# Feed-forward output product once per layer, from twelve-bit parts, accumulated in PSUM, with the gated blocks going by DRAM

## The chip, the cores and the metric

The kernel runs on one core of a Trainium2 chip. The metric is the device time of one execution in microseconds (us). Every kernel is also profiled once by the hardware profiler. The engines are named as in the profile: PE is TensorE (matrix products), PEld its weight loads, DVE is VectorE, ACT is ScalarE, POOL is GpSimd, and SP is the engine that issues most of the DMA transfers.

## The reference, cut to what matters

A graph network with four transformer layers (L = 4) over 1024 nodes of width 512. In each layer come an attention against a condition of 16 x 256 rows, and then a gated feed-forward block:

```python
for i in range(L):
    a = _attn(_ln(h, ln2_w[i], ln2_b[i]), cond, Wq[i], Wk[i], Wv[i], Wo[i])
    h = h + a
    u = _ln(h, ln3_w[i], ln3_b[i]) @ geglu_w[i] + geglu_b[i]   # 512 -> 4096
    val, gate = jnp.split(u, 2, axis=-1)
    f = val * jax.nn.gelu(gate, approximate=False)               # 1024 x 2048
    h = h + f @ ffo_w[i] + ffo_b[i]                              # 2048 -> 512
h = _gcn(h, src, dst, gcn_out_w, gcn_out_b, n)
```

The change concerns `f @ ffo_w[i]`: per layer a product of 1024 x 2048 by 2048 x 512, all in float32.

## The kernel before

It is written with a framework that records instructions in program order, allots tiles to a fixed number of buffers, adds all semaphores, and orders each engine's queue at compile time; `pin` (`keep_in_program_order`) and `in_order` fix the order of the instructions they hold. There are 36 large buffers ("slots", 128 x 1024 float32), 10 of half that size (`t512`), and eight PSUM banks of 128 x 512 float32. A tile that finds no free buffer waits until the last reader of an earlier one is done.

Two ways of multiplying float32 matrices are in use. The first is a plain float32 matmul, which shows in the profile as two records, in a Strassen-like scheme with 7 instead of 8 block products (`Quad`, `ffn_out`); its sums of blocks are computed beforehand and afterwards on DVE and POOL. The second is "twelve-bit": each operand is split into a high part, a low part and a combined part, of type fp32r, and three one-record matmuls take the place of a float32 one (`Twelve` for keys and values; `Chunk` for the gated projection). `left_parts` and `right_parts` make the parts: for 1024 columns one ACT multiplication, then DVE and POOL operations.

The feed-forward block of a layer goes through the 2048 columns of `f` in four quarters (`R = 4`, index `r`). The first quarter is made by four float32 `Quad`s (`c` = 0 to 3), while the pieces for the later quarters' right sides are split beside them: `fill()` takes one step of `begin_right` or `finish_right` at a time. The other three quarters are made by 12 `Chunk`s, whose steps are interleaved with those of the chunk before. In a chunk, `load()` fetches the geglu weights two chunks ahead (SP), `sum_chunk` adds their blocks (POOL), `split` makes their parts (ACT, DVE, POOL).

`Gated` holds one quarter of `f`, transposed, in four slots, and its Strassen sums (`sums`). As soon as a quarter is complete, `ffn_out(l, r, s, ...)` multiplies it by the quarter of `ffo_w` and adds it to the rows `h`: two calls per quarter (`s` = 0, 1, each for half of the rows), 28 float32 matmuls of 256 columns each. For `r` = 1 and 2 the two calls stand after chunks 0 and 1 of the next quarter; for `r` = 0 and 3 they follow one another. Each call's results are added to `h` and to `kept` by DVE (lines 1229, 1233 and 1245). `load_out` fetches the weights, `out_weights` makes their sums on POOL, and work for the next step is handed to `ffn_out` in `beside`. At a layer's end these are the splitting of `wk` and of `cond` for the next layer and the moments of the norm, after it that of `wv`. In the last layer it is followed by the aggregation over the graph, with `load_last` for its inputs.

The lines that matter in the profile: L1223 the matmuls of `ffn_out`; L1108 and L1170 those of a chunk (twelve-bit, and one float32 product); L296 those of the quads; L362 keys and values; L1011, L1029, L1030 the DVE work of a quad; L1042 and L1050 the steps of `begin_right` and `finish_right`; L1056 and L1059 the splitting of a chunk's left side; L1126 and L1143 a chunk's additions; L1082 a chunk's loads; L1192 and L1198 to L1200 the sums of `f`; L231 to L234 sums of blocks, among them those of `out_weights`; L313, L314, L316 `left_parts`; L324, L327, L334 `right_parts`; L759 the aggregation at the end.

Of the kernel before, what the change touches and what calls it, by code (L numbers as in the profile page):

```python
# [8 lines left out]
F32 = mybir.dt.float32  # L9
# [16 lines left out]
def gnn_kernel(  # L26
# [199 lines left out]
    cond_dram = dram.tile([NG, P, 4 * 512], F32, name="cond_dram")  # L226

# [81 lines left out]
    def left_parts(x, name):  # L309

        parts = [slots_of(2, f"{n}_{name}") for n in ("ah", "al", "as")]
        for h, l, s, x in zip(*parts, x):
            nc.scalar.mul(twelve_bits(h), x, INWARD * TINY)  # L313
            nc.vector.scalar_tensor_tensor(twelve_bits(l), h, -1.0 / TINY, x, OP.mult, OP.add)  # L314
            for k in range(2):
                nc.gpsimd.tensor_tensor(twelve_bits(s)[:, k, :], h[:, k, :], l[:, k, :],  # L316
                                        OP.subtract)
        return parts
# [643 lines left out]
    def load_out(l, r):  # L962
        return load_w(ffo_w[l][r * D:(r + 1) * D, :], f"wff_{l}_{r}")

# [12 lines left out]
    class Quad:  # L977
# [25 lines left out]
        def rest(self, fill):  # L1003
# [26 lines left out]
            pin(nc.vector.scalar_tensor_tensor(f1, d, bias, g1, OP.add, OP.mult))  # L1030
            fill()
# [35 lines left out]
    class Chunk:  # L1067
# [69 lines left out]
        def steps(self, sum_next):  # L1137
# [38 lines left out]
            pin(nc.vector.scalar_tensor_tensor(f1, d, bias, g1, OP.add, OP.mult))  # L1176

    class Gated:


        def __init__(self, l, r):
            self.n, self.tiles, self.s = f"{l}_{r}", [], None
# [6 lines left out]
        def sums(self, c, t=nc.vector, each=lambda ins: ins):  # L1189
            if c < 2:  # L1190
                a11, a21 = self.of(c)
                each(t.tensor_tensor(a21, a11, a21, OP.subtract))  # L1192
                return
            if c == 2:
                self.s = slots_of(3, f"fs_{self.n}")
            (a11, a21), (a12, a22) = self.of(c - 2), self.of(c)
            s1, s2, s4 = (x[:, c % 2, :] for x in self.s)
            each(t.tensor_tensor(s2, a22, a21, OP.subtract))  # L1198
            each(t.tensor_tensor(s1, s2, a11, OP.add))
            Gated.last = each(t.tensor_tensor(s4, a12, s2, OP.subtract))  # L1200

        def left(self):
            blocks = [[self.of(2 * j + k)[i] for k in range(2)] for i in range(2) for j in range(2)]
            return order7(blocks, *([x[:, k, :] for k in range(2)] for x in self.s))
# [5 lines left out]
    def ffn_out(l, r, s, left, right, kept, each=lambda ins: ins, beside=()):  # L1210

        n = f"{l}_{r}_{s}"
        u = kept[s]
        a, b, c, d = (bank(f"{x}_{n}") for x in ("fa", "fb", "fc", "fd"))
        h11, h12, h21, h22 = (hall[:, 4 * i + 2 * s:4 * i + 2 * s + 2, j * M:(j + 1) * M]
                              for i in range(2) for j in range(2))

        def product(i, to, start):  # L1220
            for q in range(2):
                for k in range(2):
                    each(nc.tensor.matmul(to[:, q * M:(q + 1) * M],  # L1223
                                          left[i][k][:, (2 * s + q) * P:(2 * s + q + 1) * P],
                                          right[i][:, k, :], start=start and q == 0 and k == 0,
                                          stop=q == 1 and k == 1, skip_group_check=True))

        def add(to, of):
            each(nc.vector.tensor_tensor(to, halves_of(of), to, OP.add))

        product(0, a, True)
        if r:
            each(nc.vector.tensor_tensor(u, a, u, OP.add))  # L1233
            for do in beside[2:3]:
                do()
        else:
            nc.scalar.copy(u, a)
        product(6, c, True)
        add(h22, c)
        product(4, d, True)  # L1240
        add(h22, d)
        for do in beside[3:]:
            do()
        product(5, b, True)
        each(nc.vector.tensor_tensor(u, b, u, OP.add))
        if r == R - 1:
            for to in (h22, h21, h12):
                add(to, u)
        for do in beside[:1]:
            do()  # L1250
        product(1, a, False)
        add(h11, a)
        for do in beside[1:2]:
            do()
        product(3, c, False)
        add(h21, c)
        product(2, d, False)
        add(h12, d)
# [134 lines left out]
    def load_last():  # L1393
        w = load_w(gcn_out_w, "w_out")
        pairs = slots_of(NB // 2, "base")
        for i, pair in enumerate(pairs):
            nc.sync.dma_start(pair, base_dram[2 * i:2 * i + 2].rearrange("n p d -> p n d"))
# [9 lines left out]
        return w, [pairs[nb // 2][:, nb % 2, :] for nb in range(NB)], again, row  # L1407
# [3 lines left out]
    with tc.issue_after(load_w.last.ins):  # L1411
        for d in range(NB):
            nc.sync.dma_start(c_dram[:, :, d, :].rearrange("s p n -> p s n"), by_sources(C[d]))
    for l in range(L):
# [217 lines left out]
        kept = [t512(f"kept_{l}_{i}") for i in range(2)]  # L1632
        raw_out = load_out(l, 0)
# [15 lines left out]
        def all_parts():  # L1649
            for i in (0, 1, 5, 6, 4, 3):  # L1650
                yield from begin_right(f"gt_{l}_{i}", *begun[i])
                if i < 2:
                    yield from finish_rights(i)
# [7 lines left out]
        for c, q in enumerate(quads):  # L1661
            q.rest(fill)
            if c == 0:
                with waiting_for(q.last, mybir.EngineType.Pool):
                    wff = out_weights(nc.gpsimd, l, 0, raw_out)
            f.sums(c, nc.gpsimd if c < 3 else nc.vector, pin)
        for _ in parts:
            pass
# [15 lines left out]
        load()  # L1684
        sum_chunk(0)
        def finish(*of):
            for _ in finish_rights(*of):
                pass

        def split_both():  # L1690
            split(0, False)
            split(0, True)

        finish(5)
        ffn_out(l, 0, 0, f.left(), wff, kept, pin, (lambda: finish(6), split_both))
        load()
        sum_chunk(1)
        ffn_out(l, 0, 1, f.left(), wff, kept, pin,
                (lambda: finish(4), lambda: (finish(3), split(1, False))))
        load()  # L1700
        raw_out = load_out(l, 1)

        def split_next(n):
            split(n, False)
            load()

        before = None
        for r in range(1, R):
            for c in range(KC):
                chunk = ready.pop(0)  # L1710
                flow = chunk.steps(lambda: sum_chunk(1))
                chunk.f = f if c else Gated(l, r)
                next(flow)
                if c > 2 or r == 1 and c or r > 1 and c == 0:
                    split_next(0)
                for step in range(3):
                    if before:
                        next(before, None)
                        if step == 2 and c == 0:
                            f.sums(KC - 1, nc.vector, pin)  # L1720
                    next(flow)
                output = r > 1 and c < 2
                if not output:
                    split(0, True)
                if c:
                    f.sums(c - 1, nc.vector, pin)
                before = flow
                if c == 0:
                    kept_f, f = f, chunk.f
                if output:  # L1730
                    ffn_out(l, r - 1, c, kept_f.left(), wff, kept, pin,
                            (lambda: split(0, True), lambda: split_next(1)))
                    if c == 1:
                        raw_out = load_out(l, r)
                if c == (KC - 1 if r + 1 < R else KC - 2):
                    wff = out_weights(nc.gpsimd, l, r, raw_out)
        for _ in range(3):
            next(before, None)
        f.sums(KC - 1, nc.vector, pin)
        fT = f.left()  # L1740
        if last:
            w_out, base, again, dinv_row = load_last()
            with waiting_for(Gated.last, mybir.EngineType.Pool):
                w_out = out_weights(nc.gpsimd, L, 0, w_out)
            ffn_out(l, R - 1, 0, fT, wff, kept)
        else:
            raw_wk = load_w(Wk[l + 1], f"wk_{l + 1}")
            load_cond(l + 1, 0)
            raw_wv = load_w(Wv[l + 1], f"wv_{l + 1}")
            wk = [[], [], []]  # L1750

            def split_wk(i):
                for part, t in zip(wk, right_parts(raw_wk[i:i + 1], f"wk_{l + 1}_{i}")):
                    part.extend(t)

            half = [0, 1, 4, 5], [2, 3, 6, 7]
            with in_order(mybir.EngineType.DVE):
# [19 lines left out]
    for nb in (0, 1, 4, 5):  # L1777
        into_parts(nb)
# [132 lines left out]
```

## Time and profile before

| | |
|---|---|
| median of 3 runs | 2386.01 us (2385.27 to 2387.61) |
| the profiled execution: its time | 2384.85 us |
| its span, first to last instruction | 2383.1 us |
| mean granted TensorE clock | 1.000 |
| DMA traffic | 138.32 MB, mean 58 GB/s |

How to read the rows that follow in the prediction. The page's first part gives each engine's busy time, its share of the span, and its instructions. A row of the grouped view names line, engine, operation, out<-in by tile names, shape and count; then the group's busy time and the mean of one in ns; then the idle time of the engine just before, and what ended it. A row of the view of one line gives for a group the least, median and greatest duration in ns. A row of the timeline gives start and length in us of neighbouring instructions of one kind, merged; matmuls overlap, so the distance of two starts is the time that the first one costs. A row of the view by windows gives the window, its length, and the busy time of PE, PEld and (without a filter by line) DVE, ACT and POOL with their counts, the granted clock, the mean share of the DMA engines and GB/s. A row of the waits gives who waited for whom, the sum in us, the number and the longest. A row of DMA issues gives the transfers, KB of each, and the median us from issue to landing.

### The profile page before, as it was taken

How to read it: one execution, taken by the hardware profiler on the slowest of the kernel's cores; microseconds unless marked ns; L12 is line 12 of the kernel's file. 1: busy time of each engine (PE TensorE's matmuls, PEld its weight loads, DVE VectorE, ACT ScalarE, POOL GpSimd, SP SyncE). 2: the span in 40 equal slices, each digit the busy share in tenths (PEclk: the TensorE clock that was granted, in tenths of full speed). 3: DMA queues.
4: the chain of work that ended last, by engine and by line, in shares of the span. 5: the costliest groups of instructions: out<-in, count | busy, mean ns of one | idle time of the engine just before them, and what ended most of it. 6: DMA issues, size and time to landing. Idle time of an engine off the chain costs nothing. (4 is left out here: it accounts for less than half of the span.)

```text
span 2383.1 us, 33689 instructions
## 1 busy us (share of the span) xinstructions
PE 2351.5 (99%) x12528; PEld 1769.3 (74%) x12528; DVE 1571.1 (66%) x3052; ACT 994.5 (42%) x2011; POOL 919.0 (39%) x815
## 2 busy tenths in 40 slices
PE   8999999999999999999999999999999999999999
PEld 5668886677777887577786888477786888567787
DVE  9874546887684455877794544867786544778764
ACT  7444444343344444343344444433334444434320
POOL 0142223565222224564512323555523224356531
PEclk9999999999999999999999999999999999999999
DMA  6041210111301101011211201021121111011140
GB/s 203 18 157 71 72 67 19 45 45 53 111 27 67 41 30 43 22 58 54 83 37 67 67 19 54 10 62 45 45 93 67 46 39 36 19 54 40 49 151 36
DMA packets 108844, 138.32 MB, mean 58 GB/s; under 512 B 8232, under 2 KB 65904, under 8 KB 108672
## 3 DMA queue, kind: packets, MB, share of 16 engines
q1 hardware_dynamic: 106576, 130.64, 17.0%
q0 software_dynamic: 1376, 4.30, 0.5%
q8 instruction: 104, 1.70, 0.3%
q10 hardware_dynamic: 720, 1.11, 0.1%
q14 instruction: 68, 0.56, 0.1%
HBM read 119.25 MB, written 16.78 MB: 57 GB/s over the span
## 5 line engine op out<-in xcount | busy, mean ns | idle before, releaser
L316 POOL TENSOR_TENSOR as_c<-ah_c,al_c 128x512 fp32r<-128x512 f32 x128 | 187.8, 1497 | 235.0 <-DVE al_c L314 228.9
L1122 ACT ACTIVATE g<-g 128x512 f32<-128x512 f32 x192 | 112.1, 584 | 280.0 <-PE g L1108 277.4
L373 ACT ACTIVATE v<-v 128x512 f32<-128x512 f32 x127 | 74.1, 584 | 220.5 <-PE v L362 218.3
L1059 POOL TENSOR_TENSOR gsa<-gha,gla 128x512 fp32r<-128x512 f32 x96 | 125.8, 1331 | 104.1 <-DVE gla L1056 104.1
L1059 POOL TENSOR_TENSOR gsb<-ghb,glb 128x512 fp32r<-128x512 f32 x48 | 70.1, 1461 | 218.6 <-DVE glb L1056 218.6
L362 PE MATMUL v<-bh_wv,ah_c 128*128 128x512 f32 x508 | 145.9, 409 | 0.0
L362 PE MATMUL v<-bs_wv,as_c 128*128 128x512 f32 x508 | 143.4, 404 | 0.0
L843 ACT ACTIVATE pr<-sc,nmax 128x256 f32<-128x256 f32 x256 | 118.1, 474 | 58.3 <-DVE nmax L838 58.3
L1108 PE MATMUL g<-gr,gsa 128*128 128x512 f32 x384 | 136.5, 436 | 0.0
L362 PE MATMUL v<-bl_wv,al_c 128*128 128x512 f32 x508 | 136.4, 390 | 0.0
L1135 ACT ACTIVATE g<-g,gcols 128x512 f32<-128x512 f32 x96 | 67.5, 703 | 164.8 <-DVE g L1143 161.6
L373 ACT ACTIVATE k<-k 128x512 f32<-128x512 f32 x125 | 72.6, 585 | 150.6 <-PE k L362 150.4
L362 PE MATMUL k<-ah_c,bh_wk 128*128 128x512 f32 x500 | 135.1, 392 | 0.0
L362 PE MATMUL k<-al_c,bl_wk 128*128 128x512 f32 x500 | 133.9, 390 | 0.0
L362 PE MATMUL k<-as_c,bs_wk 128*128 128x512 f32 x500 | 132.2, 395 | 0.0
L915 POOL TENSOR_TENSOR os<-oT 128x256 f32<-128x256 f32 x12 | 8.8, 734 | 318.8 <-DVE oT L889 291.5
L1223 PE MATMUL fa<-wff,fT 128*128 128x256 f32 x512 | 121.9, 381 | 6.7 <-DVE kept L1233 6.7
L1108 PE MATMUL g<-gr,gha 128*128 128x512 f32 x384 | 122.9, 401 | 0.0
L1108 PE MATMUL g<-gl,gla 128*128 128x512 f32 x384 | 119.0, 391 | 0.0
L1223 PEld LDWEIGHTS fa<-wff,fT 128*128 128x128 f32 x512 | 96.6, 190 | 26.7 <-DVE kept L1233 9.9
L378 DVE COPY kT<-k 128x512 f32<-128x512 f32 x54 | 37.3, 691 | 118.4 <-PE k L362 118.4
L362 PEld LDWEIGHTS v<-bs_wv,as_c 128*128 128x128 f32 x508 | 93.9, 188 | 24.2 <-issue 4.6
(368 smaller groups left out, 5875.6 us busy)
## 6 DMA issues: line engine op xcount, KB each, us to landing
ct<-cond_dram SPq DMA_DIRECT2D x48, 512.0 KB, 4.5
wff<-in_L_gnn_ffo_w_dram SPq DMA_DIRECT2D x32, 512.0 KB, 4.3
gxb<-in_L_gnn_geglu_w_dram SPq DMA_DIRECT2D x96, 128.0 KB, 2.2
gxa<-in_L_gnn_geglu_w_dram SPq DMA_DIRECT2D x96, 128.0 KB, 2.2
cond<-in_L_gnn_cond_dram SPq DMA_DIRECT2D x32, 256.0 KB, 3.5
cond_dram<-ct SPq DMA_DIRECT2D x16, 512.0 KB, 3.9
wk<-in_L_gnn_Wk_dram SPq DMA_DIRECT2D x8, 512.0 KB, 6.1
wv<-in_L_gnn_Wv_dram SPq DMA_DIRECT2D x8, 512.0 KB, 8.4
```

The lines of the kernel that those rows point to most:

```text
L316: nc.gpsimd.tensor_tensor(twelve_bits(s)[:, k, :], h[:, k, :], l[:, k, :], OP.subtract)
L362: pin(nc.tensor.matmul(self.bank, twelve_bits(left[k // 2])[:, k % 2, self.c * P:(self.c + 1) * P], twelve_bits(right[k // 2])[:, k % 2, : ...
L373: nc.scalar.mul(self.bank, self.bank, 1.0 + TINY)
L378: nc.vector.tensor_copy(self.to(), self.bank)
L843: nc.scalar.activation(pr3[:, a, :], ps3[:, a, :], AF.Exp, bias=nmax[:, a:a + 1], accum_out=tot[:, a:a + 1])
L915: t.tensor_tensor(s1, a21, a22, OP.add)
L1059: pin(nc.gpsimd.tensor_tensor(s_at, h_at, l_at, OP.subtract))
L1108: pin(nc.tensor.matmul(to, self.part(i, which)[:, k, :], self.rights[i][which].bitcast(F32R)[:, k, :], start=start and k == 0, stop=stop a ...
L1122: pin(nc.scalar.mul(to, to, 1.0 + TINY))
L1135: pin(nc.scalar.activation(to, of, AF.Gelu, bias=gcols[:, cg:cg + 1]))
L1223: each(nc.tensor.matmul(to[:, q * M:(q + 1) * M], left[i][k][:, (2 * s + q) * P:(2 * s + q + 1) * P], right[i][:, k, :], start=start and q ...
```

## The change

`ffn_out` with its Strassen sums goes, and so do `load_out` and the uses of `kept` and of `out_weights` for the layers. A class `Output` multiplies all of `f` by all of `ffo_w` once a layer, after the last chunk, without Strassen, from twelve-bit parts. Each finished block of `f` is stored to DRAM (`f_dram`) by two SP transfers. The output then runs over 16 units: two halves `s` of the rows by eight pairs of inner blocks. A unit fetches 512 KB of `f`, splits it (ACT once, DVE twice over 1024 columns), and multiplies 4 blocks of 128 rows. Each block of rows has two banks, `y` and `x`, that accumulate over all eight units; at the end of a half, DVE adds them to `h` with two operations per block. The weights' parts (24 slots) are made once and serve both halves: two of eight pairs during the last chunks, the others one per unit by `ahead`. The work for the next layer that stood beside `ffn_out` stands after units 8 to 14. In the first quarter, each piece of the right sides is now finished right after it is begun, and the first chunk is loaded after quad 1 and split after quad 2.

```diff
+    f_dram = dram.tile([2, DFF // P, P, 2, 256], F32, name="f_dram")
...
-    def left_parts(x, name):
+    def left_parts(x, name, t=None):
...
             nc.scalar.mul(twelve_bits(h), x, INWARD * TINY)
             nc.vector.scalar_tensor_tensor(twelve_bits(l), h, -1.0 / TINY, x, OP.mult, OP.add)
+            if t:
+                t.tensor_tensor(twelve_bits(s), h, l, OP.subtract)
+                continue
...
-        def sums(self, c, t=nc.vector, each=lambda ins: ins):
...
+        def store(self, c):
+            for s in range(2):
+                nc.sync.dma_start(f_dram[s, self.r * KC + c],
+                                  self.tiles[c][:, :, s * M:(s + 1) * M])
...
-    def ffn_out(l, r, s, left, right, kept, each=lambda ins: ins, beside=()):
...
+    class Output:
...
+        def fetch(self, n):
+            if n < 2 * UNITS:
+                s, u = divmod(n, UNITS)
+                self.raw[n] = slot(f"fr_{self.l}_{n}")
+                nc.sync.dma_start(self.raw[n], f_dram[s, 2 * u:2 * u + 2].rearrange(
+                    "c p i n -> p c (i n)"))
+        def split(self, n):
+            if n in self.raw:
+                self.f[n] = left_parts([self.raw.pop(n)], f"f_{self.l}_{n}", nc.vector)
...
+        def split_w(self, u):
+            x, name = self.raw_w.pop(u), f"wff_{self.l}_{u}"
+            h, l, s = self.w[u] = [slot(f"{n}_{name}") for n in ("bh", "bl", "bs")]
+            nc.scalar.mul(twelve_bits(h), x, INWARD / TINY)
+            yield
+            for k in range(2):
+                pin(nc.vector.scalar_tensor_tensor(
+                    twelve_bits(l)[:, k, :], x[:, k, :], 1.0 / TINY, h[:, k, :], OP.mult,
+                    OP.subtract))
+                yield
+                pin(nc.vector.scalar_tensor_tensor(
+                    twelve_bits(s)[:, k, :], h[:, k, :], -TINY, l[:, k, :], OP.mult, OP.add))
+                yield
...
+        def unit(self, n):
+            s, u = divmod(n, UNITS)
+            left, right = self.f.pop(n), self.w[u]
+            for b in range(4):
+                if u == 0:
+                    self.banks[b] = [bank(f"{x}_{self.l}_{s}_{b}") for x in ("fy", "fx")]
+                y, x = self.banks[b]
+                for which, to in enumerate((y, y, x)):
+                    for k in range(2):
+                        pin(nc.tensor.matmul(
+                            to, twelve_bits(left[which][0])[:, k, b * P:(b + 1) * P],
+                            twelve_bits(right[which])[:, k, :],
+                            start=u == 0 and which != 1 and k == 0,
+                            stop=u == UNITS - 1 and which != 0 and k == 1, skip_group_check=True))
+                if u == UNITS - 1:
+                    to = h[4 * (b // 2) + 2 * s + b % 2]
+                    nc.vector.scalar_tensor_tensor(to, y, 1.0 + TINY, to, OP.mult, OP.add)
+                    nc.vector.tensor_tensor(to, x, to, OP.add)
...
         def all_parts():
-            for i in (0, 1, 5, 6, 4, 3):
+            for i in SPLIT:
                 yield from begin_right(f"gt_{l}_{i}", *begun[i])
-                if i < 2:
-                    yield from finish_rights(i)
+                yield from finish_rights(i)
...
+        fetches = [(R - 2, 0), (R - 2, 3), (R - 1, 1), (R - 1, 3)]
+        splits = {(R - 2, 1): 3, (R - 2, 2): 2, (R - 1, 0): 3, (R - 1, 1): 2}
...
+            beside = {8: lambda: (fetch_next(), take_moments(l + 1, half[0], 0, 2)),
+                      9: lambda: split_of(wk, raw_wk, "wk", 0),
+                      10: lambda: split_of(wk, raw_wk, "wk", 1),
+                      11: lambda: (norm_first(), fetch_values()),
+                      12: lambda: split_cond(l + 1, 0),
+                      13: lambda: split_of(wv, raw_wv, "wv", 0),
+                      14: fetch_more}
+        with in_order(mybir.EngineType.DVE):
+            for n in range(2 * UNITS):
+                output.fetch(n + 2)
+                output.split(n + 1)
+                output.fetch_w(n + 4)
+                for _ in range(5):
+                    next(ahead, None)
+                output.unit(n)
+                beside.get(n, nothing)()
+            if not last:
+                split_of(wv, raw_wv, "wv", 1)
```

In the last layer the units 8, 9 and 13 are followed instead by the first half of the aggregation's parts (`into_parts`), by the fetch of the graph's counts (`load_counts`, POOL transfers into eight slots) and by that of the output weights; `load_base` follows the last parts.

237 lines of the change are left out of this document (96 added, 141 removed).

## The prediction

> **What bounds the kernel now.** I read the busy shares first.
>
> ```profile
> PE 2351.5 (99%) x12528; PEld 1769.3 (74%) x12528; DVE 1571.1 (66%) x3052; ACT 994.5 (42%) x2011; POOL 919.0 (39%) x815
> PEclk9999999999999999999999999999999999999999
> ```
>
> TensorE is busy 99% of the span at the full granted clock, and VectorE, the next engine, 66%. A change is therefore worth what it takes from TensorE's stream, less what TensorE newly waits for. Next come TensorE's waits (times in all, how often, the longest).
>
> ```profile
> PE fa L1223 <- DVE kept L1233: 6.7, 8, 0.8
> PE fd L1223 <- DVE fs L1199: 3.5, 8, 0.4
> PE gc L296 <- DVE gu L1011: 3.2, 4, 0.8
> PE g L1108 <- DVE g L1126: 1.0, 3, 0.3
> ```
>
> Line 1223 is the feed-forward output product, line 296 in these rows the gated projection's first quarter, line 1108 the chunks of the other three quarters. Three of the four waits stand at code that the change rewrites. Since matmuls overlap, I take their price from starts, not from busy time: the timeline of one call of `ffn_out` that waits, and line 1223's busy time by windows (all, a pair of calls, a waiting call, one that does not wait, another pair).
>
> ```profile
> 1072.85 1.89 PE L1223 MATMUL fa<-wff,fT 128*128 128x256 f32 x8
> 1074.57 1.89 PE L1223 MATMUL fc<-wff,fT 128*128 128x256 f32 x8
> 1076.30 0.59 PE L1223 MATMUL fd<-wffs,fs 128*128 128x256 f32 x2
> 1077.33 1.56 PE L1223 MATMUL fd<-wffs,fs 128*128 128x256 f32 x6 [0.43 <-DVE fs L1199]
> 1078.73 1.89 PE L1223 MATMUL fb<-wffs,fs 128*128 128x256 f32 x8
> 1081.45 1.99 PE L1223 MATMUL fa<-wff,fT 128*128 128x256 f32 x8 [0.83 <-DVE kept L1233]
> ...
> 1086.55 0.81 PE L1108 MATMUL g<-gr,gha 128*128 128x512 f32 x2
> ```
>
> ```profile
> 0.00:2383.10 2383.10, 395.12 (x1792) 338.88 (x1792) 1.00 0.18 58
> 1001.50:1025.60 24.10, 24.07 (x112) 21.02 (x111) 1.00 0.28 84
> 1072.80:1086.70 13.90, 12.58 (x56) 10.29 (x56) 1.00 0.14 39
> 1096.60:1108.70 12.10, 12.01 (x56) 10.51 (x56) 1.00 0.41 132
> 1197.60:1221.80 24.20, 24.14 (x112) 21.10 (x111) 1.00 0.10 36
> ```
>
> One of the seven products, four float32 matmuls of 256 columns at two records each, takes 1.73 us from start to start (1072.85 to 1074.57). A waiting call takes 1086.55 - 1072.85 = 13.70 us; busy 12.58 plus waits of 1.26 would be 13.84, so 0.1 of a call's busy time lies under its neighbour, and a call that does not wait is worth 12.01 - 0.1 = 11.9, a pair 24.0.
>
> **The change, part by part.**
>
> *TensorE, removed.* A layer has two pairs (first and last quarter), two waiting calls and two others: 2 x 24.0 + 2 x 13.70 + 2 x 11.9 = 99.2 us, in four layers 396.8. The row over the whole span, 395.1, agrees.
>
> *TensorE, added.* A layer has 16 units (two halves of the rows, eight pairs of inner blocks), each 4 blocks of rows x 3 parts x 2 = 24 twelve-bit matmuls of 512 columns: 384 a layer, 1536 in all. This operation is in the trace, in the chunks:
>
> ```profile
> 1028.10 0.63 PE L1108 MATMUL g<-gr,gha 128*128 128x512 f32 x2
> ...
> 1036.77 0.62 PE L1108 MATMUL g<-gr,gsb 128*128 128x512 f32 x2
> ```
>
> These are the first and the last of 20 rows of two matmuls: 38 matmuls in 8.67 us, 0.228 each, with nothing idle between. The new product costs 1536 x 0.228 = 350.5 us, 87.6 a layer and 5.48 a unit. TensorE's account is 350.5 - 396.8 = -46.3 us. The 0.228 holds only while its inputs are there, so the rest is a question of supply.
>
> *First quarter, gained.* `out_weights` and the Strassen sums of `f` leave GpSimd, which slows VectorE here:
>
> ```profile
> 978.44 1.71 POOL L231 TENSOR_TENSOR wffs<-wff 128x512 f32<-128x512 f32 x1
> 985.15 2.96 POOL L1192 TENSOR_TENSOR fT<-fT 128x512 f32<-128x512 f32 x2
> 987.50 1.16 DVE L1042 SCALAR_TENSOR_TENSOR gr<-ln3T,gt 128x512 fp32r<-128x512 f32 x1
> 989.19 0.67 DVE L1042 SCALAR_TENSOR_TENSOR gr<-ln3T,gt 128x512 fp32r<-128x512 f32 x1
> ```
>
> One form takes 1.16 us beside GpSimd and 0.67 without, and that lag makes the 0.8 us wait at `gc` once a layer. Eight of the twelve `finish_right` operations move from the first output calls into this stage, and the first chunk's split with them.
>
> ```profile
> L1011 DVE TENSOR_TENSOR gd<-gd,gu 128x512 f32<-128x512 f32 x16 | 11.1, 695 | 7.4 <-PE gd L296 7.4
> L1030 DVE SCALAR_TENSOR_TENSOR fT<-gd,gcols,g 128x512 f32<-128x512 f32 x16 | 11.8, 739 | 0.0
> ```
>
> ```profile
> 983.22 1.88 PE L296 MATMUL gb<-ln3S,ges 128*128 128x512 f32 x4
> 984.93 1.88 PE L296 MATMUL gc<-ln3T,wgate 128*128 128x512 f32 x4
> ```
>
> A quad on VectorE is then at most 5 additions and 5 fills at 0.69 and two of 0.74: 8.4 us against TensorE's 5 products at 984.93 - 983.22 = 1.71, 8.6. I book the 3.2 us as gained; if GpSimd's chunk sums keep the lag alive, it is 0.
>
> *Chunks, 0.* Additions and splits stay. VectorE loses the Strassen sums there and gets ten steps of weight splitting. The `f` stores, two a chunk, join SP's queue: behind a store that waits for `f1` stand the next chunk's loads, due a whole chunk later. If that margin goes, I allow up to 0.2 us a chunk, 10 in all, in the range only.
>
> *Output stage, supply.* VectorE and ScalarE must split each `f` unit and, up to unit 5, one pair of weight blocks. No such tile exists now; the nearest rows are the same code on other tiles.
>
> ```profile
> L314 DVE SCALAR_TENSOR_TENSOR al_c<-ah_c,ct x64: 1211/1217/2284, 100.1 to 1998.5; 128x1024 fp32r<-128x1024 f32 x64
> L1056 DVE SCALAR_TENSOR_TENSOR gla<-gha,gxa x48: 1211/1434/2312, 459.3 to 2275.5; 128x1024 fp32r<-128x1024 f32 x48
> L327 DVE SCALAR_TENSOR_TENSOR bl_wk<-wk,bh_wk x16: 679/683/1002, 94.9 to 1763.7; 128x512 fp32r<-128x512 f32 x16
> L313 ACT ACTIVATE ah_c<-ct 128x1024 fp32r<-128x1024 f32 x2 | 2.0, 1045 | 0.0
> ```
>
> (The first three give least, median and greatest ns.) A unit costs VectorE 2 x 1.22 + 4 x 0.68 = 5.2 us and ScalarE 2 x 1.05 = 2.1, under 5.48. At the contended 1.43 it would be 5.6, over by 0.1. I take the quiet price, because GpSimd has only four operations in this stage (`split_cond`). In the second half the weights are done; instead come eight accumulator reads of 0.69 (5.5), twelve pieces of `wk` and `wv` at 0.68 (8.2), two of `cond` at 1.22 (2.4), and moments and roots, which I estimate at 5, beside 8 x 2.44 = 19.5: 41 us against 43.8. It fits, narrowly. All eight PSUM banks belong to one half, but a block's two reads (1.4 us) match its six matmuls (1.37), so the second half can follow on.
>
> *DMA.* `f` goes out and back, 8.4 MB each way a layer, and in the first eight units 1 MB (`f` and weights) must land per unit, 1.05 MB / 5.48 us = 191 GB/s.
>
> ```profile
> ct<-cond_dram SPq DMA_DIRECT2D x48, 512.0 KB, 4.5
> wff<-in_L_gnn_ffo_w_dram SPq DMA_DIRECT2D x32, 512.0 KB, 4.3
> 2298.00:2312.00 14.00, 14.00 (x61) 11.27 (x60) 12.60 (x18) 1.41 (x2) 5.35 (x4) 1.00 0.93 337
> ```
>
> The last row (DMA share 0.93, 337 GB/s) shows room, and a fetch is issued two units, 11 us, ahead of a chain of 4.5 + 1.05 + 2.44 = 8.0 us. So 0, as long as a slot is free.
>
> *Seams, a loss.* After the last chunk `f0`, an addition and `f1` still stand on VectorE ahead of `split(1)`, and SP holds the last store ahead of `fetch(2)`. From the chunk's end I count 1.7 for those, 2.4 for `split(1)`, 2.7 for weights: the second unit is ready at 4.1 against 5.48, the third at about 9.3 against 11. Lower bound 0, upper one whole chain of 8; nearer the count, 1 us a layer, 4 in all. In the last layer 4 MB of counts join the fetches on the same DMA engines: 0 to 5, I take 2.
>
> **Sum.** The profiled execution took 2384.85 us (span 2383.1, 1.75 around it). 2384.85 - 46.3 - 3.2 + 4 + 2 = 2341.3. The median of the three runs is 1.2 higher, 2386.0, so I predict 2342 us, 44 us or 1.8% faster.
>
> **Rivals.** (A) *VectorE becomes the bound.* If GpSimd's work keeps its two-input operations at the contended price through the output stage (1.43, and 1.16 for 0.68), each of the first six units costs 2 x 1.43 + 4 x 1.16 = 7.5, 2.0 over, and the second half 5.5 + 12 x 1.16 + 18 x 1.43 + 5 = 50.2 against 43.8, 6.4 over: 18 us a layer, 74 in all, 2416; at half the overlap, 2379. For it: the 1.16 us row. Against: GpSimd is left with some 6 us in that stage. Chance 0.06, mostly at a part.
> The Trainium skill, page "SBUF — State Buffer", section "Who interferes with whom", says that a VectorE operation with two SBUF inputs and a reading GpSimd operation exclude each other completely. By that rule a 0.68 us operation behind a 1.71 us one would take up to 2.4, not the 1.16 seen, so the trace shows the conflict but not the whole of that price; it speaks against this change, which swaps accumulator additions for splits with two SBUF inputs.
>
> (B) *The slots run short, and the kernel gets slower.* Of 36 slots I count 24 for weight parts, 6 for `f` parts, 2 raw, 4 for the next layer at unit 8: exactly 36. If one is held longer, SP's queue stops at a fetch until the unit before has ended, and the fetch has one unit instead of two: 8.0 - 5.48 = 2.5 us of stall for each unit so hit. All 64 make 2342 + 160 = 2502; from 18 units on (44 / 2.5) the kernel is slower than before. For it: loads now wait for slots already.
>
> ```profile
> SPq L1082 <- PE g L1108: 399.1, 36, 21.9
> ```
>
> Against: the count closes at 36, and before and after unit 8 it is lower. Chance 0.09; a few units hit only cost 5 to 15.
>
> (C) *Every seam costs a whole chain*, 8 us instead of 1, because SP's store holds the fetches: 2342 + 28 = 2370. Chance 0.10. (D) *The product is no cheaper than it was*, since 190 ns of weight load per matmul are not hidden: 2342 + 1536 x 0.19 = 2634. The chunk rows load just as often at 0.228, so 0.01.
>
> **How the numbers follow.** The forecast has 0.74, with its own range 2334 (no seams at all: 2386 - 46.3 - 3.2 - 1.0, the `g` wait gone too, is 2335.5) to 2352. For eight in ten I go on to (C) and to small parts of (A) and (B): 2332 to 2364. About 0.2%, 4.8 us, is what a measurement of this kernel tells from no change. Faster: 0.74 + 0.10 and the parts of (A) and (B) that stay small, 0.02 each, together 0.88; within it 0.03, where these two eat the gain; slower 0.09, the rest of (A), 0.02, of (B), 0.06, and (D).
>
> **What would show it.** Right: 1536 new matmuls starting 0.228 apart with few waits; the `kept`, `fs` and `gc` waits gone; VectorE busy over 85% in the output stage without TensorE idle; 67 MB more of DMA bytes. Wrong: TensorE waiting in units for `f` parts (A, if VectorE is busy then; B, if a fetch or SP is late), or 5 to 8 us idle at the first units (C). A next layer that starts late, for want of `wk` or the norm, would be a miss of a step that I price at nothing.

## The result, and the profile after

The changed kernel takes 2390.49 us in the median of 13 runs (2388.59 to 2393.04); the kernel before took 2385.85 us in as many runs beside them (2384.96 to 2387.61). The ratio is 1.002, with a 95% interval of 1.0011 to 1.0028: 4.6 us slower, where 44 us faster was forecast. The profiled execution took 2390.05 us, its span is 2388.3.

The page of the changed kernel, its busy shares and the DMA bytes:

```profile
PE 2324.4 (97%) x12272; PEld 1722.9 (72%) x12272; DVE 1585.6 (66%) x3024; ACT 1082.1 (45%) x2099; POOL 794.7 (33%) x731
DMA packets 161068, 205.42 MB, mean 86 GB/s; under 512 B 11304, under 2 KB 101744, under 8 KB 160896
```

TensorE has 27 us less to do and stands idle longer. The waits of TensorE say for whom:

```profile
PE g L1110 <- ACT g L1124: 35.7, 20, 6.9
PE gc L297 <- DVE gu L1012: 6.3, 4, 1.6
PE g L1110 <- DVE g L1128: 3.0, 8, 0.4
PE fx L1255 <- DVE as_f L317: 2.0, 4, 0.5
```

(L1110 is the chunks' matmul that was L1108, L297 the quads', L1255 the new output product; L1124 scales a chunk's sums on ScalarE.) The `kept` and `fs` waits are gone. The `gc` wait doubled from 3.2 to 6.3, and a wait that was not there before, the chunks' for ScalarE, holds 35.7 us. The longest of these, 6.6 to 6.9, comes four times, once a layer.

To divide the whole difference I take, for every matmul record of a line, the distance to the next record's start, and set idle gaps above 0.15 us apart:

| stage (line before / after) | before, us | after, us | difference |
|---|---|---|---|
| output product (L1223 / L1255) | 386.6 + 10.2 waits | 351.4 + 2.0 waits | -43.4 |
| chunks, twelve-bit (L1108 / L1110) | 417.6 + 1.0 waits | 429.7 + 38.7 waits | +49.8 |
| chunks, float32 product (L1170 / L1172) | 64.6 | 63.1 | -1.6 |
| quads (L296 / L297) | 383.2 + 3.2 waits | 381.3 + 6.3 waits | +1.2 |
| all others | | | -0.9 |

The differences add up to 5.1, and the two profiled executions differ by 2390.05 - 2384.85 = 5.2. The product brought what it should; the same 1728 matmuls of the chunks cost 50 us more, 37.7 of them in waits and 12.1 in longer matmuls.

The windows of the second layer show where (columns as in the prediction): the first chunk in three parts, then the output stage.

```profile
1002.70:1014.60 11.90, 5.23 (x22) 3.65 (x21) 6.72 (x11) 4.21 (x8) 2.85 (x4) 0.90 0.47 136
1014.60:1019.10 4.50, 4.47 (x11) 3.54 (x12) 2.85 (x5) 0.36 (x1) 4.10 (x5) 0.51 0.02 5
1019.10:1023.57 4.47, 4.47 (x21) 3.68 (x20) 1.89 (x4) 3.90 (x7) 2.56 (x3) 1.00 0.00 0
1135.58:1223.87 88.29, 87.80 (x387) 72.16 (x386) 81.55 (x106) 27.19 (x27) 8.32 (x4) 1.00 0.49 170
```

And the first chunk of the kernel before:

```profile
1025.50:1037.23 11.73, 11.73 (x52) 9.50 (x51) 5.88 (x10) 6.63 (x12) 6.70 (x7) 1.00 0.16 45
```

The first chunk takes 20.87 us (1002.70 to 1023.57) instead of 11.73. TensorE is busy for 5.23 of the first 11.90 us, and then runs for 4.5 us at half the clock. In four layers that is 4 x 9.14 = 36.6 of the 49.8. The output stage, 88.29 us long with TensorE busy for 87.80, is as forecast.

What TensorE waits for in this chunk is read from the timelines backwards. TensorE, ScalarE, GpSimd, SP's queue and VectorE, in this order:

```profile
1007.32 0.61 PE L1110 MATMUL g<-gl,gla 128*128 128x512 f32 x2
1014.62 1.19 PE L1110 MATMUL g<-gr,gsa 128*128 128x512 f32 x2 [6.69 <-ACT g L1124]
```

```profile
1005.15 0.58 ACT L1124 ACTIVATE g<-g 128x512 f32<-128x512 f32 x1 [0.35 <-PE g L1110]
1012.46 1.06 ACT L1057 ACTIVATE gha<-gxa 128x1024 fp32r<-128x1024 f32 x1 [6.73 <-POOL gxa L1094]
1013.89 1.07 ACT L1124 ACTIVATE g<-g 128x512 f32<-128x512 f32 x2
```

```profile
1010.23 0.72 POOL L1094 TENSOR_TENSOR gxa<-gxa,gxb 128x256 f32<-128x256 f32 x1 [8.53 <-DMA gxa<-in_L_gnn_geglu_w_dram]
```

```profile
997.29 4.23 SPq L1084 DMA_DIRECT2D gxb<-in_L_gnn_geglu_w_dram  x4
1005.39 1.19 SPq L1194 DMA_DIRECT2D f_dram<-fT  x2
1006.68 2.16 SPq L1084 DMA_DIRECT2D gxa<-in_L_gnn_geglu_w_dram  x4
```

```profile
1004.63 0.74 DVE L1031 SCALAR_TENSOR_TENSOR fT<-gd,gcols,g 128x512 f32<-128x512 f32 x1
```

The last quad's piece of `f` is done at 1005.37 (1004.63 + 0.74). SP's queue holds the store of that piece (L1194) ahead of the second chunk's wide load `gxa` (L1084), so the load is issued at 1006.68 and has landed by 1010.23. GpSimd sums it, and ScalarE's next instruction in order is the wide split of the *second* chunk, at 1012.46; the first chunk's scaling (L1124), whose input had long been there, stands behind it, and TensorE needs its bank. One store that waits for its data stops an engine that is two queues away. In the kernel before, the second chunk's load stood at no store, and its split not inside the first chunk: between the quads and the first chunk stood the two output calls of the first quarter, 24.1 us of TensorE work (1001.50 to 1025.60 in the prediction's windows), and that split was made beside them. The change takes this stretch away.

### The profile page after: what moved, and what is told of

Its sections match the earlier page's. It is cut to its first block, busy times and chain, and to the rows that moved or that the text cites. A ratio compares the mean times of both kernels' runs of the same rounds, so it can differ in the third digit from the quotient of the medians.

```text
span 2388.3 us, 33592 instructions
## 1 busy us (share of the span) xinstructions
PE 2324.4 (97%) x12272; PEld 1722.9 (72%) x12272; DVE 1585.6 (66%) x3024; ACT 1082.1 (45%) x2099; POOL 794.7 (33%) x731
## 2 busy tenths in 40 slices
DMA packets 161068, 205.42 MB, mean 86 GB/s; under 512 B 11304, under 2 KB 101744, under 8 KB 160896
## 3 DMA queue, kind: packets, MB, share of 16 engines
q8 instruction: 102, 1.67, 0.3%
## 5 line engine op out<-in xcount | busy, mean ns | idle before, releaser
L320 POOL TENSOR_TENSOR as_c<-ah_c,al_c 128x512 fp32r<-128x512 f32 x128 | 195.3, 1556 | 416.8 <-PE fy L1255 242.1
L1110 PE MATMUL g<-gr,gsa 128*128 128x512 f32 x384 | 142.0, 452 | 35.7 <-ACT g L1124 35.7
L1255 PE MATMUL fx<-bs_wff,as_f 128*128 128x512 f32 x512 | 158.2, 390 | 2.0 <-DVE as_f L317 2.0
L1255 PE MATMUL fy<-bh_wff,ah_f 128*128 128x512 f32 x512 | 159.3, 392 | 0.0
L1255 PE MATMUL fy<-bl_wff,al_f 128*128 128x512 f32 x512 | 157.7, 389 | 0.0
L1124 ACT ACTIVATE g<-g 128x512 f32<-128x512 f32 x192 | 110.3, 581 | 99.3 <-PE g L1110 97.2
L314 ACT ACTIVATE ah_f<-fr 128x1024 fp32r<-128x1024 f32 x64 | 67.5, 1060 | 174.9 <-PE fy L1255 116.3
L1137 ACT ACTIVATE g<-g,gcols 128x512 f32<-128x512 f32 x96 | 67.5, 704 | 132.4 <-DVE g L1145 129.9
L1110 PEld LDWEIGHTS g<-gr,gsa 128*128 128x128 f32 x384 | 72.4, 194 | 76.1 <-issue 61.8
L1110 PE MATMUL g<-gr,gha 128*128 128x512 f32 x384 | 121.0, 396 | 0.0
L1110 PE MATMUL g<-gl,gla 128*128 128x512 f32 x384 | 118.8, 390 | 0.0
```

The costliest lines, as they stand in the source:

```text
L1110: pin(nc.tensor.matmul(to, self.part(i, which)[:, k, :], self.rights[i][which].bitcast(F32R)[:, k, :], start=start and k == 0, stop=stop a ...
L1124: pin(nc.scalar.mul(to, to, 1.0 + TINY))
L1137: pin(nc.scalar.activation(to, of, AF.Gelu, bias=gcols[:, cg:cg + 1]))
L1255: pin(nc.tensor.matmul(to, twelve_bits(left[which][0])[:, k, b * P:(b + 1) * P], twelve_bits(right[which])[:, k, :], start=u == 0 and whic ...
```

## The experiments

Each is the changed kernel with the edit shown, and its time is compared with the kernel before, run on the same chip beside it. My theory: the order of the queues at the seam from the quads to the chunks. The rival: VectorE is the bound there, or the new output stage costs what was lost.

**1. The second chunk's wide split behind the first chunk's steps**

```diff
-                split(0, False)
+                first = (r, c) == (1, 0)
+                if not first:
+                    split(0, False)
...
+                if first:
+                    split(0, False)
```

> Only the place of one call is changed: the wide half of the second chunk's split (ACT gha, DVE gla, POOL gsa) is issued after the first chunk's steps, not between its first two. Theory 1 (ACT's queue is in order, and the second chunk's gha, whose block sums on POOL are late, stands in front of the first chunk's copy gs and of the scaling): the 6.7 us wait of g for ACT in the first chunk goes in all four layers, with the slow clock behind it (0.51 for 4.5 us); the first chunk takes 11.7 to 12.5 us and not 20.9, and a smaller wait of 1 to 2 us may appear at the second chunk: some 28 to 36 us less, 2355 to 2363 us. Theory 2 (the late loads themselves hold the chunks, whatever stands in front of what): the wait moves to the second chunk in full, time within 5 us of 2390. Theory 3 (VectorE is behind with the right sides' pieces): no change.

Measured: 2381.43 us, ratio 0.9989 (0.9977 to 1.0), between the two expectations. The wait of the first chunk is gone, and one stands at the start of the second:

```profile
PE g L1110 <- ACT gha L1057: 13.1, 4, 4.2
```

So ScalarE's order made the first chunk wait, but taking it away only uncovers the late load behind it.

**2. The last quad's store behind the second chunk's wide load**

```diff
-            self.f.store(self.c)
+            if self.c < KC - 1:
+                self.f.store(self.c)
...
         sum_chunk(1)
+        with tc.issue_after(Chunk.wide_loaded.ins):
+            f.store(KC - 1)
```

> Only the order of SP's queue is changed: the store of quad 3's block stands behind the wide load of the second chunk. Theory 1 with the store as the cause of the lateness: the load is issued some 3 us earlier (at the end of the last quad, when a slot is freed, and not at 4 us after it), so the 6.7 us wait in the first chunk shrinks to 3 to 4 us, in all 12 to 16 us less, 2375 to 2379 us. If instead the freed slot alone sets the load, within 3 us of 2390.

Measured: 2368.17 us, 0.993 (0.9908 to 0.9953), 22 us less than the changed kernel. The wait for ScalarE falls from 35.7 to 18.8, the longest from 6.9 to 2.3 (the edit shifts these lines by one to three). The wait and SP's queue:

```profile
PE g L1113 <- ACT g L1127: 18.8, 24, 2.3
```

```profile
995.80 0.93 SPq L1085 DMA_DIRECT2D gxa<-in_L_gnn_geglu_w_dram  x2
999.58 1.19 SPq L1197 DMA_DIRECT2D f_dram<-fT  x2
```

The load now stands 3.8 us ahead of the store; in the changed kernel it stood 1.3 us behind it. VectorE's work is the same in both, so the rival does not explain this gain.

**3. Both edits together**

> Both edits together. Theory 1: no wait over 1 us in the first two chunks, 2352 to 2358 us, a few us better than the later split alone. If the later split alone already hides the loads: the same as that one within 2 us.

Measured: 2379.05 us, 0.9977 (0.9966 to 0.9988), a miss, and 11 us worse than the second alone. The late split is itself late: the second chunk waits for it, though its load is there.

```profile
PE g L1113 <- ACT gha L1058: 14.8, 4, 3.8
```

The split belongs where the changed kernel has it, if its data come in time.

**4. Three pieces of the right sides finished behind the second chunk's load.** A piece that is finished holds one more slot (`low` in `finish_right`). If that is why the load comes late, finishing only three of six ahead of it must let the load pass the store with no edit of the order.

```diff
-            for i in SPLIT:
+            for n, i in enumerate(SPLIT):
                 yield from begin_right(f"gt_{l}_{i}", *begun[i])
-                yield from finish_rights(i)
+                if n < 3:
+                    yield from finish_rights(i)
...
         sum_chunk(1)
+        for _ in finish_rights(*SPLIT[3:]):
+            pass
```

> Half of the moved finishing steps goes back behind the quads: three of six low parts (three slots, six VectorE operations) are made after the last quad. Theory 1: the slots are free earlier, the second chunk's wide load stands ahead of quad 3's store, and the wait at the first chunk shrinks by 2 to 4 us a layer; the wait at gc (1.6 us) shrinks to 0.8 or less because VectorE has less to do: together 10 to 20 us less, 2370 to 2380 us. If slots are not what the load waits for: only the gc part, 3 us less, 2387.

Measured: 2363.18 us, 0.9909 (0.988 to 0.9938), 27.3 less than the changed kernel. SP's queue of this kernel:

```profile
991.43 0.93 SPq L1084 DMA_DIRECT2D gxa<-in_L_gnn_geglu_w_dram  x2
998.31 1.19 SPq L1194 DMA_DIRECT2D f_dram<-fT  x2
```

The load is issued 7 us ahead of the store, and the 6.7 us wait in the first chunk is gone, more than was expected. What is left is another wait, of 1.5 us, at the start of the second chunk (1007.52; the first begins at 995.67): ScalarE's activation (L1137) waits there 4.11 us for VectorE's additions, which come after the six finishing steps (998.20 to 1001.89). The `gc` wait, which was expected to shrink, stayed at 6.2 us.

**5. The steps of the weights' splitting at each chunk's end, on top of 4.** Most of the remaining waits for ScalarE lie in the chunks that split output weights between their own steps (`ahead`).

```diff
-        splits = {(R - 2, 1): 3, (R - 2, 2): 2, (R - 1, 0): 3, (R - 1, 1): 2}
+        splits = {(R - 2, 1): 2, (R - 2, 2): 2, (R - 2, 3): 1, (R - 1, 0): 2, (R - 1, 1): 2, (R - 1, 2): 1}
...
-                    if step < splits.get((r, c), 0):
-                        next(ahead)
                 split(0, True)
+                for _ in range(splits.get((r, c), 0)):
+                    next(ahead)
```

> On top of the run with half of the finishing steps put back (2363 us): the ten weight-splitting steps of the chunk stage are issued at a chunk's end, at most two a chunk, and not between its steps. Theory (VectorE's two to three extra operations delay a chunk's g1, the gelu of it waits at the head of ACT's queue, and the next chunk's scaling behind it): the four waits of 0.3 to 0.75 us a layer go, 11 us less, 2352 us. Rival (VectorE is simply full in these chunks): they move to other places, 2360 to 2364 us.

Measured: 2350.68 us, 0.9853 (0.9825 to 0.9882), 12.5 less than 4. The row of the waits was `15.2, 21, 1.5` in 4 and is now:

```profile
PE g L1110 <- ACT g L1124: 5.9, 4, 1.5
```

ScalarE's activation ahead of that scaling (L1137) waits for an addition of VectorE, in the changed kernel (first row) longer than here (second):

```profile
1070.47 0.73 ACT L1137 ACTIVATE g<-g,gcols 128x512 f32<-128x512 f32 x1 [3.26 <-DVE g L1145]
1064.02 0.73 ACT L1137 ACTIVATE g<-g,gcols 128x512 f32<-128x512 f32 x1 [2.17 <-DVE g L1145]
```

The steps between (L1232, L1236) are VectorE's: they delay its addition, and the scaling stands behind in ScalarE's order, as the theory said.

**6. The narrow half of the first chunk's split behind the last quad, on top of 4.** Meant to take the `gc` wait, since that split stands on VectorE among the last quad's additions.

```diff
-                split(0, True)
         for _ in parts:
             pass
+        split(0, True)
         load()
```

> On top of the same run: the narrow half of the first chunk's split stands behind quad 3 and not ahead of it. Theory (the 1.6 us wait at gc comes from the first chunk's split, 1.75 us of VectorE time and its GpSimd part, standing ahead of quad 3's first addition): the wait shrinks from 1.6 to 0.6 to 0.9, and 3 to 4 us in all, 2359 us; if it comes from the right sides' pieces, it stays at 1.6.

Measured: 2391.6 us, 1.0021 (1.0008 to 1.0033), 28.4 more than 4. The `gc` wait shrinks from 1.56 to 1.24 us each; but the narrow buffer is held longer, the next load waits for it, and the store is ahead again. SP's queue, then the waits:

```profile
998.77 1.09 SPq L1084 DMA_DIRECT2D gxa<-in_L_gnn_geglu_w_dram  x2
1007.58 1.19 SPq L1194 DMA_DIRECT2D f_dram<-fT  x2
1008.87 2.17 SPq L1084 DMA_DIRECT2D gxb<-in_L_gnn_geglu_w_dram  x4
```

```profile
PE g L1110 <- ACT g L1124: 33.4, 20, 6.1
PE gc L297 <- DVE gu L1012: 5.0, 4, 1.2
```

A miss in time, and a strong confirmation: another buffer, the same order, the same 6 us wait, the same loss.

**7. The conditioning difference in the output stage on VectorE, on top of 4**

```diff
-            conds[g] = left_parts(raw_x.pop((l, g)), f"c_{l}_{g}")
+            conds[g] = left_parts(raw_x.pop((l, g)), f"c_{l}_{g}", nc.vector if l and not g else None)
```

> On top of the same run: the difference of the two parts of cond in the output stage is taken by VectorE (two operations of 1.2 us) and no longer by GpSimd (four of 1.5). Theory (a two-input operation of VectorE stands still while GpSimd holds the shared ports): al_f and as_f there fall from 2.1 to 2.3 us to 1.22, bl_wv and bs_wv from 1.7 to 0.69; VectorE does 2.4 us more and is held 4 us less, the wait at as_f (0.5 us) goes, 2361 us. If the long durations are not GpSimd's, they stay, and the wait grows to 2 us or more.

Measured: 2360.92 us, 0.9896 (0.9867 to 0.9925), 2.3 less than 4, within the two intervals; the rows decide. VectorE's timeline in the changed kernel, beside GpSimd's four subtractions, which run from 1206.46 to 1214.78:

```profile
1206.46 8.32 POOL L320 TENSOR_TENSOR as_c<-ah_c,al_c 128x512 fp32r<-128x512 f32 x4 [80.73 <-PE fy L1255]
```

```profile
1207.37 2.33 DVE L315 SCALAR_TENSOR_TENSOR al_f<-ah_f,fr 128x1024 fp32r<-128x1024 f32 x1
1209.80 2.12 DVE L317 TENSOR_TENSOR as_f<-ah_f,al_f 128x1024 fp32r<-128x1024 f32 x1
1211.85 1.78 DVE L331 SCALAR_TENSOR_TENSOR bl_wv<-wv,bh_wv 128x512 fp32r<-128x512 f32 x1
1213.66 1.67 DVE L338 SCALAR_TENSOR_TENSOR bs_wv<-bh_wv,bl_wv 128x512 fp32r<-128x512 f32 x1
1215.25 0.68 DVE L331 SCALAR_TENSOR_TENSOR bl_wv<-wv,bh_wv 128x512 fp32r<-128x512 f32 x1
```

With the difference on VectorE the same four operations take 1.22, 1.23, 0.69 and 0.69 us, `al_f` falls from 1285 to 1220 ns in the mean, and the waits for `as_f` from 2.0 to 0.5 us. So the long durations were GpSimd's. Rival (A) exists, and is worth no more than that.

**8. As 4, but four pieces finished ahead of the load** (`n < 4`, `SPLIT[4:]`)

> On top of the same run: four instead of three low parts are finished in the quads (one more slot in use there, two VectorE operations fewer in the first chunk). Theory (what is left of the first chunk's wait, 1.5 us, is VectorE with its six finishing operations): it shrinks to under 0.8, 3 us less, 2360 us; if slots decide, the second chunk's load is late again and the time rises by 4 us or more.

Measured: 2368.36 us, 0.9927 (0.9899 to 0.9956), 5.2 more than 4, though the intervals overlap; the waits are those of experiment 2:

```profile
PE g L1110 <- ACT g L1124: 18.4, 24, 2.0
```

SP's queue is that of experiment 2 as well: the load is issued at 995.68, 3.8 us ahead of the store (999.47), and not 7. The wait in the first chunk is back, with 2.0 us, and in one layer a stretch at half the clock follows it. So one more slot held makes the load late again.

**9 to 12. The three gains together, with two pieces finished inside the first chunk.** All have 5 and 7; `n < 2` or `n < 3` pieces are finished ahead of the load, `SPLIT[2:4]` or `SPLIT[3:4]` behind it, and:

```diff
+                    if (r, c) == (1, 0) and step < 2:
+                        for _ in finish_rights(SPLIT[4 + step]):
+                            pass
```

In the last two, `output.split(0)` also moves from behind the last chunk into its first step.

> This is the changed kernel with three edits together: the product's right parts of two pieces finished ahead of the second chunk's wide load, two behind it and two more inside the first chunk; the early inner products at the end of each chunk; the conditioning difference in the output stage on VectorE. My theory (queue order and slots at the seam, in-order ACT): the three gains were 27.3, 12.5 and 2.3 us where each was taken alone, so about 2348 to 2349 us; if finishing fewer pieces ahead of the load also takes VectorE out of the wait of the gated sum at the seam (1.56 us in each layer), up to 6 us less, 2342. The rival (VectorE is the bound of the seam, work moved along it only comes back later) expects the two pieces inside the first chunk to come back there as waits for VectorE: 2352 or more.

> As the version with two pieces, but with three pieces finished ahead of the second chunk's wide load, one behind it and two inside the first chunk. My theory expects 2348 to 2350 us, the waits of the seam as they were with the early inner products at the chunks' ends alone (1.5 to 1.6 us each for the gated sum and for the first chunk), and none for VectorE in the output stage. The rival expects 2352 or more.

> As the version with three pieces, but the output stage's first own split of the left side is issued inside the layer's last chunk, no longer behind it. My theory expects that the start of the output stage no longer waits for it, at most 1 us in each layer: 2344 to 2349 us. The rival expects the last chunk to wait for VectorE instead, 2350 or more.

> As the version with two pieces, but the output stage's first own split of the left side is issued inside the layer's last chunk, no longer behind it. My theory expects the sum of what both edits give, 2340 to 2348 us; the rival 2350 or more.

Measured: 2357.22 (0.9884, 0.9868 to 0.9901), 2355.41 (0.9874, 0.9858 to 0.9891), 2357.49 (0.9881, 0.9865 to 0.9898) and 2357.37 (0.9885, 0.9869 to 0.9902). All four missed, and the times are those of the rival; in the first two the new wait is the rival's too. The waits of the second:

```profile
PE g L1110 <- DVE gl L1052: 8.0, 12, 1.1
PE gc L297 <- DVE gu L1012: 6.2, 4, 1.6
```

The `gc` wait did not move, and TensorE now waits for VectorE's low parts (L1052), which in this order run beside GpSimd. VectorE and GpSimd in the second, then VectorE in experiment 5, where the same operation runs alone (each row holds two operations):

```profile
999.06 2.37 DVE L1052 SCALAR_TENSOR_TENSOR gl<-ln3T,gr 128x512 fp32r<-128x512 f32 x2
```

```profile
999.22 3.36 POOL L1061 TENSOR_TENSOR gsa<-gha,gla 128x512 fp32r<-128x512 f32 x2 [2.85 <-DVE gla L1058]
```

```profile
998.00 1.29 DVE L1052 SCALAR_TENSOR_TENSOR gl<-ln3T,gr 128x512 fp32r<-128x512 f32 x2
```

Splitting the left side earlier gave nothing: the wait for ScalarE at L1124 grew from 3.5 and 3.4 to 6.1 us, while that for VectorE at L1128 fell from 3.0 to 1.3, so the profile does not show the wait for VectorE that the rival named.

**13. Without the pieces inside the first chunk.** 5 and 7 and nothing else: it differs from the second of these four only in where those two pieces are finished.

> As the version with three pieces, but the two pieces that were finished inside the first chunk are finished behind the second chunk's wide load again; the early inner products at the chunks' ends and the conditioning difference on VectorE stay. If the pieces inside the first chunk cost what was lost there (VectorE holds up that chunk's low parts), this gives what the edits gave where each was taken alone: 2350.7 less 2.3, 2347.5 to 2349.5 us, with no wait for the low parts in the first chunk. If it is the conditioning difference on VectorE that holds up the chunks, it stays at 2353 to 2357.

Measured: 2347.78 us (2347.52 to 2348.74), 0.9841 (0.9828 to 0.9855): a version that beats both kernels, 38 us or 1.6% under the kernel before. There is no wait for low parts; the largest waits that are left from the quads on:

```profile
PE gc L297 <- DVE gu L1012: 6.2, 4, 1.6
PE g L1110 <- ACT g L1124: 6.0, 4, 1.5
PE g L1110 <- DVE g L1128: 3.0, 8, 0.4
```

## Why the prediction was wrong

- **TensorE removed and added: right.** 396.8 and 353.4 us against 396.8 and 350.5; the matmuls start 0.229 apart (351.4 / 1536), against 0.228.
- **Output stage and DMA: right.** VectorE is busy for 81.55 of 88.29 us, 92%, and TensorE waits for `as_f` for 0.5 us a layer. The traffic grew by 67.1 MB (138.32 to 205.42).
- **Seams of the output stage: too dear.** 4 and 2 were booked; with all its waits the product came out 2.9 above 350.5, which is what all its seams cost in line 1255.
- **"Chunks, 0": the step that failed, by 48 us** (49.8 less 1.6 in the float32 product). The prediction said that behind a store that waits for `f1` "stand the next chunk's loads, due a whole chunk later". At the first chunk this is not so: the 24 us of output product that stood ahead of it are gone, and the second chunk's split now stands inside the first chunk, so its load is due within half of that chunk. The 0.2 us a chunk kept for the range was the wrong kind of bound: a load behind such a store is late by a chain (store, load, sums, split), 6.7 us here, and not by an issue. The first chunks make 36.6 of the 49.8 us. The same step booked the ten steps of weight splitting as harmless: VectorE takes them ahead of an addition that ScalarE waits for, and the scaling that TensorE needs stands behind. Experiment 5 shows 12.5 us for it.
- **"First quarter, gained 3.2": wrong in sign, +3.1 in the `gc` wait** (+1.2 for the quads as a whole). GpSimd's sums left, but the first chunk's split came in, and stands between the last quad's additions. The timeline of VectorE in the changed kernel:

```profile
995.40 1.22 DVE L1058 SCALAR_TENSOR_TENSOR gla<-gha,gxa 128x1024 fp32r<-128x1024 f32 x1
996.54 0.68 DVE L1058 SCALAR_TENSOR_TENSOR glb<-ghb,gxb 128x512 fp32r<-128x512 f32 x1
997.14 0.68 DVE L1012 TENSOR_TENSOR gu<-gb,gs 128x512 f32<-128x512 f32 x1
```

  The count of a quad left out these 1.9 us, though it names the split among what moves there. Half of the finishing taken out of the quads left the wait as it was (experiment 4). Experiment 6 took a part of the split away and 0.3 us of the 1.56; that the rest of it makes up the wait is argued, not shown.
- **The rivals.** (B) named the mechanism, slots that run short and SP's queue that stops, but counted the slots for the output stage alone. It struck at the quads' end, once a layer, where six finished pieces and two chunks' loads meet; experiments 4, 6 and 8 show it. (C) named the other half, a store on SP that holds the loads behind it for a whole chain, but at the output's first units, where TensorE did not stop. (A) was worth 2.0 us in all, the waits for `as_f`. (D) fell with the price.
- **What was missed in addition:** the half clock behind each long wait. Of the 12.1 us in longer matmuls some 10 lie in the first chunks (8.5 us of matmuls before, 11.0 after, in each layer).

With the seam mended, experiment 13 lands 5.8 us above the forecast. Its own waits come near that: `gc` 6.2 instead of 0, 6.0 at the second chunk's start, 3.0 instead of 1.0 at L1128, 14.2 together, less 5.4 that the output's seams were booked too high and 3.5 in the quads and the chunks' float32 product: 5.3. What the output product should bring was read rightly; what the change moved in the queues was not.

## What to carry to other kernels

A transfer that waits for a computed result is a barrier for every later one in its queue: for each load behind it, ask when its first consumer comes up in *that engine's* order, not when its product is needed. Count the buffers at the point where most are held, which may be far from the stage that is rewritten. Here work for a later stage did better behind the instructions that free TensorE's banks than between them (experiment 5).

## What the hardware showed that was not expected

After an idle stretch of 6.69 us TensorE's granted clock was 0.51 for 4.5 us, and pairs of matmuls started 0.85 us apart (1016.47 to 1017.32) instead of 0.47 (1019.02 to 1019.49):

```profile
1016.47 1.05 PE L1110 MATMUL g<-gl,glb 128*128 128x512 f32 x2
1017.32 1.05 PE L1110 MATMUL g<-gr,gsa 128*128 128x512 f32 x2
1019.02 0.63 PE L1110 MATMUL g<-gl,glb 128*128 128x512 f32 x2
1019.49 0.62 PE L1110 MATMUL g<-gr,gha 128*128 128x512 f32 x2
```

After the 4.25 us of experiment 1 the next 4.5 us ran at 0.50, and after the 1.5 us of experiment 4 at 1.00. Between these the length of the wait alone does not decide. In experiment 8 two waits of 1.96 us at the same place, in the third and the fourth layer, were followed by these windows (columns as before, the clock is the third number from the end):

```profile
1551.45:1555.95 4.50, 4.50 (x13) 3.61 (x14) 3.79 (x7) 0.98 (x3) 3.12 (x3) 0.64 0.29 85
2099.16:2103.66 4.50, 4.50 (x20) 3.70 (x21) 4.31 (x7) 0.99 (x3) 3.13 (x3) 1.00 0.31 89
```

Over these 4.5 us 13 matmuls ran in the first and 20 in the second. So a wait can cost more than itself, and one of 2 us already may. The Trainium skill, page "TensorE: Matmul & The Clock Gate", section "Part 1: The HAM clock gate (the "warmup" mystery)", gives half the clock after an idle window of about 3.4 us, and 427 ns for 512 columns at it. The trace agrees with the second (0.85 / 2 = 0.425). The first fits the waits of 1.5, 4.25 and 6.69 us, but not the first of these two of 1.96 us; why it halved the clock and the other did not stays open.

Beside GpSimd a VectorE operation of 0.68 us took 1.67 to 1.78 and one of 1.22 took 2.12 and 2.33 (experiment 7). The prediction held that the trace shows the conflict "but not the whole of that price" of the Trainium skill, page "SBUF — State Buffer", section "Who interferes with whom"; these rows show operations slowed by 0.9 to 1.1 us each, and experiment 7 takes the slowing away with GpSimd's operations, so they lie nearer to the exclusion that the page states. The prediction read its own rows too mildly: the operation of 1.16 us began at 987.50, 0.6 us ahead of the end of GpSimd's (985.15 + 2.96 = 988.11), so exclusion would make it about 0.6 + 0.67 = 1.3 (an estimate, as the profile's spans on GpSimd are rough), and its row for `al_c` had a greatest duration of 2284 ns beside a median of 1217. Here it still cost only 2 us, since the units around them had the slack.
